# Turning routing scores and the first expert's rows on VectorE instead of TensorE, in a cross-attention and mixture-of-experts kernel

## The chip, the cores and the metric

The kernel runs on one core of a Trainium2 chip. The metric is device time in microseconds (us) of one execution; the time of a kernel is the median of several executions. A profile is one execution taken by the hardware profiler. Its times count from the first instruction, and its span ends with the last one.

The engines are named as the profile names them: PE is TensorE's matmuls and PEld its weight loads, DVE is VectorE, ACT is ScalarE, POOL is GpSimd, and SP is SyncE, which here only issues DMAs. Each engine works through its own instructions in order and waits on semaphores for the others.

## The reference

The kernel computes one transformer block in fp32: `x` is 32 sequences of 100 tokens with 512 features. Cut to what matters:

```python
x = x + xattn(layernorm(x), ctx, ctx)      # 16 heads, causal mask, softmax over the keys, + bias
h = layernorm(x)                           # 3200 tokens x 512
scores = softmax(h @ gate_w.T)             # per token, over 16 experts
topk_w, topk_idx = top_k(scores.T, 12)     # each expert takes its 12 best tokens of each sequence
x_tok = h[topk_idx]
eo = (gelu(x_tok @ Wg.T) * (x_tok @ Wu.T)) @ Wd.T * topk_w     # per expert, hidden size 1024
shared = (gelu(h @ Ws_g.T) * (h @ Ws_u.T)) @ Ws_d.T            # for all tokens
out = x + scatter_add(eo) + shared
```

Because of the causal mask over 100 queries, only the first 100 of 722 context positions matter.

## The kernel before

**Precision.** Every fp32 product of matrices is made of three matmuls. A value is split into a high part (ScalarE copies it to a rounded fp32 type) and a low part (VectorE subtracts the high part from the value), and `mm3` (L49) multiplies high by high, high by low and low by high. So every operand needs one ScalarE and one VectorE instruction before TensorE can use it.

**Attention** runs in 32 units (`u`), four for each of eight blocks of 400 tokens. A unit does, for four heads: the scores of the unit before, the query projection, the turns of the softmax of two units before, a K projection of 384 tokens, in three units out of four also a V projection, and the values of two units before. Units 8, 12 and 16 have no V projection and are shorter on TensorE ("short units"). The softmax passes through VectorE (maxima, L254), GpSimd (subtraction, L263), ScalarE (exponential, L267), VectorE again (sum, L272) and GpSimd (multiplication, L278); ScalarE also copies the turned softmax out (`pt`, L289). The order in each unit is written out by hand in the loop at L543, and each engine keeps it.

Beside that, the four 128-row slices of the output projection's weights are loaded (`load_w`) and split (`fc_split`, L672: L674 on ScalarE, L675 on VectorE), one in each of the units 9 to 12 (`FC_AT`). After them the bias, a table of bases and the router's weights are loaded (`load_consts`, L658, unit 13), and the router's weights are split (`split_consts`, L666, unit 15: L669 and L670).

**Feed-forward** comes next. `job` (L804) runs one expert over up to 384 tokens: eight chunks `f` of the hidden size; in each, `gate_up_mm` (24 matmuls for gate and 24 for up, tile `gu`), then `hidden` (L773 gelu on ScalarE, L774 product on VectorE, L777 and L778 the split of the result), then `down` of the chunk before (tile `dn`). Extra work is hung on a chunk `f`: the list `mid` is issued between gate/up and `down`, the list `post` after `down`. `at(post, 3, ...)` means "after chunk 3's `down`". Within one chunk, calls are issued in the order in which they were added.

First the shared expert runs over eight groups of tokens (`g` from 0 to 7; a ninth group is kept for the end). While a group runs, the next one is prepared (`Prep`): output projection, residual, layer norm, store of the normalized rows to `xn` in DRAM (tensor `xnD`, L1069), turn of the rows so that features lie on partitions (`turn_pe`, L962, four TensorE transposes for 128 rows; or `turn_dve`, L972), and router logits, which end as rows of `LG`, one of 25 tiles of 128 tokens by 16 experts each.

**Routing** (`Route`). In group 6 the softmax over the first 20 tiles is taken after chunk 1. The scores are then turned so that each expert's 3200 scores lie in a row: `turn` (L1191) makes one TensorE transpose for a tile (L1201) and one VectorE copy for up to four of them (L1202), and stores to `sD` in DRAM (L1205). The 20 tiles are spread over chunks 3, 4 and 6 of group 6. The last five tiles get their softmax after chunk 7, and their turn in chunk 0 of group 7. Then `load` (L1213) reads the scores back with 4 rows of 100 for each partition, `top` (L1222 to L1226) finds the 12 best, `exchange` (L1235 to L1242) passes values and indices through DRAM, and `slots` (L1249, L1256) turns them on TensorE into a weight, a row index (`isl`) and a quarter-row index (`iq`) for each slot.

**Experts.** Each of the 16 has 384 slots, in three tiles. `gather` (L934) fetches their rows from `xn`. For the experts after the first this takes four indirect DMAs for each tile, each fetching quarter rows of 128 features (L948), so that the tile arrives as 32-row blocks; `turn_dve` then needs a blockwise 32x32 transpose on VectorE (L979), and the split (L980 on ScalarE, L981 on VectorE). Their three turns are hung on chunks 4, 5 and 6 of the expert before. The first expert's rows come as whole rows (L943, one DMA for each tile) and are turned by TensorE in chunk 7 of group 7 (`turn_pe`, L968, split by L969 and L970). An expert's weights come in eight chunks (`wraw`, L718 on SP), which `chunk_split` splits (L742 on ScalarE, L743 on VectorE) during the expert before. The results are added to the output by indirect DMAs (L991).

Tiles come from pools with a fixed number of buffers: `big` has one, `gx` three. A new tile waits until all uses of the old one are over.

Of the kernel before, what the change touches and what calls it, by code (L numbers as in the profile page):

```python
# [16 lines left out]
T = B * S  # L17
# [8 lines left out]
KSTART = [sum(KVB[:j]) for j in range(len(KVB))]  # L26
KMAX = 384
KS = 1
FC_AT = 9
BUF = dict(cr=4, raw=6, cx=8, x=4, v=2, kk=2, kt=2, vt=2, q=3, p=5, pt=5, y=2, pj=2, sc=1, tr=2)  # L30
GROUPS = [3, 2, 3, 3, 3, 3, 3, 3, 2]
GMAX = 384
# [28 lines left out]
def attention(tc, K, F):  # L61
    nc = tc.nc
    with ExitStack() as ctx, ExitStack() as kvctx:
# [477 lines left out]
        with tc.manual_schedule(engines={mybir.EngineType.Pool}):  # L541
            prologue()
            for u in range(NU - 3):  # L543
                sb, c = divmod(u, NC4)
                a, back = u - 1, u - 2
                a = a if a >= 0 else None
                back = back if back >= 0 else None
                j, ck = divmod(u - KS, NC4)
                j += 2
                kv = j in blocks  # L550
                vv = kv and ck < KVB[j]
                jn, d = divmod(u + NC4 - KS, NC4)
# [12 lines left out]
                if FC_AT <= u < FC_AT + NC4:  # L565
                    fr = load_w(3, u - FC_AT)
                if u == FC_AT + NC4:
                    F.load_consts()
                if u == FC_AT + NC4 + 2:
                    F.split_consts()  # L570
                if a is not None:
                    scores(a)
                if u - 3 >= 0:
                    y_keep(u - 3)
                if a is not None:
                    sm_max(a, 0)
                    sm_sub(a, 0)
                    sm_max(a, 1)
                    sm_sub(a, 1)
                qkeep(u, qproj(u))  # L580
                if a is not None:
                    sm_exp(a, 0)
                if back is not None:
                    p_turn(back, 0)
                    p_turn(back, 1)
                    p_keep(back, 0)
                    p_keep(back, 1)
                if xn:
                    x_stats(*xn)
                if a is not None:  # L590
                    sm_exp(a, 1)
                    sm_sum(a, 0)
                    sm_mul(a, 0)
                pk = kproj(j, ck) if kv else None
                if kv and vv:
                    kkeep(j, ck, pk)
                if c == 1:
                    vload(sb)
                if back is not None:
                    p_turn(back, 2)  # L600
# [12 lines left out]
                if FC_AT <= u < FC_AT + NC4:  # L613
                    F.fc_split(u - FC_AT, fr)
                if u == 0:
                    vkeep(1, 1, vproj(1, 1))
                if vv:
                    vkeep(j, ck, vproj(j, ck))
                if xs:
                    x_turn(sb + 1, c, vv)  # L620
                if back is not None:
                    values(back)
# [8 lines left out]
class FeedForward:  # L631
# [4 lines left out]
    def __init__(self, tc, K, top):  # L636
# [15 lines left out]
        self.sel = self.base[:, 5:5 + NE]  # L652
        self.gr = wfp.tile([128, NC4, 32], F32, name="gr")
        self.gw = wfp.tile([128, NC4, 64], FR, name="gw")
        self.LG = wfp.tile([128, T // 128, NE], F32, name="LG")
        self.stacks = [top.enter_context(ExitStack()) for _ in range(3)]

    def load_consts(self):  # L658
# [3 lines left out]
        nc.gpsimd.memset(gr, 0.0)  # L662
        nc.sync.dma_start(gr[:, :, 0:NE], K.gwT)
        nc.gpsimd.memset(f32(gw), 0.0)

    def split_consts(self):  # L666
        nc, gw, gr = self.nc, self.gw, self.gr
# [150 lines left out]
    def run(self):  # L818
# [10 lines left out]
        for g in range(ng):  # L829
# [58 lines left out]
            if g == ng - 2:  # L888
                n = self.starts[ng - 1]
                at(post, 1, lambda n=n: Route.softmax(self, 0, n))  # L890
                at(post, 3, lambda: r.turn(0, 4), lambda: r.turn(4, 4))
                at(mid, 4, lambda: r.turn(8, 4, True))
                at(mid, 6, lambda: r.turn(12, 4))
                at(post, 6, lambda n=n: r.turn(16, n - 16, True))
                at(post, 7, lambda n=n: Route.softmax(self, n, T // 128))
            if g == ng - 1:
                at(mid, 0, lambda n=n: r.turn(n, T // 128 - n, True))
                at(post, 0, r.load)
                at(post, 1, *[lambda j=j: r.top(j) for j in range(4)], r.exchange)
                at(post, 3, r.slots, lambda: self.gather(0, r))  # L900
                for i in range(NST):
                    at(mid, 7, lambda i=i: self.gturn(0, i))
                for f in range(1, NFC):
                    at(post, f, lambda f=f: self.chunk_split(NFC + f - 1))
            xh, xl, x1s = self.ready.pop(g)
# [28 lines left out]
    def gather(self, e, r):  # L934
# [3 lines left out]
        for j in range(NST):  # L938
            g = self.gxp.tile([128, NC4, 128], F32, name="gx")
            self.gx.append(g)  # L940
            if e == 0:
                nc.gpsimd.indirect_dma_start(
                    out=g.rearrange("p c f -> p (c f)"), out_offset=None, in_=self.K.xn,  # L943
                    in_offset=bass.IndirectOffsetOnAxis(ap=r.isl[:, j:j + 1], axis=0))
                continue
            for k in range(4):
                i = (e * NST + j) * 4 + k
                nc.gpsimd.indirect_dma_start(  # L948
# [4 lines left out]
    def gturn(self, e, j):  # L953
        if j == 0:
            self.xg = self.xt_tiles()
        if e == 0:
            self.turn_pe(self.xg, j, self.gx[j].rearrange("p c f -> p (c f)"),
                         self.ps_m.tile([128, D], F32, name="m").rearrange("p (c t) -> p c t", c=NC4))
        else:
            self.turn_dve(self.xg, j, self.gx[j])  # L960

    def turn_pe(self, x, i, rows, tv):  # L962

# [209 lines left out]
class Route:  # L1173


    def __init__(self, F):
        self.F, self.nc = F, F.nc
        self.so = None

    @staticmethod  # L1180
    def softmax(F, a, b):
# [6 lines left out]
        nc.vector.reciprocal(sm[:, 1], sm[:, 1])  # L1188
        nc.vector.tensor_tensor(LG, LG, sm[:, 1, :, None].to_broadcast([128, NT, NE]), ALU.mult)

    def turn(self, b0, nb, store=False):  # L1191
        F, nc = self.F, self.nc
        if self.so is None:
            self.so = F.bigp.tile([128, NC4, GMAX], F32, name="big").rearrange("p c t -> p (c t)")
            self.at = b0
        for t0 in range(b0, b0 + nb, 4):
            nt = min(4, b0 + nb - t0)
            o = (t0 - self.at) * 128
            tb = F.ps_m.tile([128, D], F32, name="m")
            for i in range(nt):  # L1200
                nc.tensor.transpose(tb[0:NE, i * 128:(i + 1) * 128], F.LG[:, t0 + i, :], F.K.ident)  # L1201
            nc.vector.tensor_copy(self.so[0:NE, o:o + nt * 128], tb[0:NE, 0:nt * 128])  # L1202
        if store:
            n = b0 + nb - self.at
            nc.sync.dma_start(F.K.sD[:, self.at * 128:(self.at + n) * 128],  # L1205
                              self.so[0:NE, 0:n * 128])
            self.so = None

    def load(self):
        F, nc = self.F, self.nc  # L1210
# [122 lines left out]
```

## Time and profile before

| | us |
|---|---|
| median of 3 runs | 1677.03 (1675.21 to 1677.6) |
| the profiled execution | 1675.84 |
| its span | 1674.0 |
| attention, from 62 to 345: PE busy | 279.50 of 283 |
| shared groups, from 345 to 724: PE busy | 376.02 of 379 |
| group 6 from the softmax on, 724 to 776: PE busy | 51.77 of 52 |
| group 7, 776 to 830: PE busy | 52.48 of 54 |
| experts and the late group, 830 to 1674: PE busy | 839.70 of 844 |

The granted TensorE clock is 0.999 over the span. A matmul's duration in the timeline includes the time in which it overlaps with the next one, so the time that a piece of work takes on TensorE is read from the start of the one to the start of the next. In a line of a timeline the columns are start, duration, engine, line, operation, output and inputs, shape, count, and in brackets the idle time of the engine before it and what ended that. In a line of waits the numbers are the total in us, the number of times, and the longest.

### The profile page before, as it was taken

To read this page: it belongs to the slowest core of one execution; us is meant where nothing else is said; L and a number is where in the kernel's file an instruction comes from. 1 tells how busy PE (TensorE), PEld (TensorE's weight loads), DVE (VectorE), ACT (ScalarE), POOL (GpSimd) and SP (SyncE) were. 2 spreads that over 40 slices of the span, in tenths; PEclk is the share of its full clock that TensorE was granted. 3 is DMA by queue.
4 is the path that set the end of the run, shared out by engine and by line. 5 is a ranking of instruction groups with operands and counts; after the bars stand their busy time and mean duration, and the time that the engine had idled before them with its cause. 6 is when DMAs were issued, how large, how long until landed. Compare 5 with 4: busy or idle time off the path is not lost.

```text
span 1674.0 us, 28093 instructions
## 1 busy us (share of the span) xinstructions
PE 1657.8 (99%) x10879; PEld 1523.1 (91%) x10879; DVE 917.9 (55%) x2199; ACT 679.3 (41%) x1088; POOL 625.7 (37%) x542
## 2 busy tenths in 40 slices
PE   9999999999999999999999999999999999999998
PEld 8888899879898999989899999999999999999998
DVE  5778777665433334344555555555555555555542
ACT  4555555553111111122344444444444444444442
POOL 3877777670111011010343344343344343344011
PEclk9999999999999999999999999999999999999999
DMA  7456554555322233211545555455555455555452
GB/s 236 149 166 182 161 164 151 177 181 176 114 70 76 76 101 114 82 45 42 158 163 161 160 157 164 152 152 161 161 155 160 158 150 161 161 155 164 136 160 62
DMA packets 107125, 237.47 MB, mean 142 GB/s; under 512 B 14161, under 2 KB 58418, under 8 KB 106992
## 3 DMA queue, kind: packets, MB, share of 16 engines
q1 hardware_dynamic: 93632, 209.99, 38.4%
q0 software_dynamic: 12944, 25.22, 8.0%
q8 instruction: 85, 1.39, 0.4%
q10 hardware_dynamic: 416, 0.48, 0.1%
q14 instruction: 48, 0.39, 0.1%
HBM read 181.90 MB, written 53.73 MB: 141 GB/s over the span
## 4 chain that ended last, share of the span: by engine, by line
PE 92%; POOL 2%; DVE 2%; ACT 1%; issue 1%; DMA 1%; SPq 0%; POOLq 0%; ACTq 0%; DVEq 0%
PE gu L56 49%; PE dn L56 24%; PE kv L56 10%; PE m L56 3%; PE ms L284 2%; POOL p L263 2%; PE ms L299 2%; PE sc L243 1%; DVE p L254 1%; ACT pt L289 1%; DMA raw<-wA 1%; PE ms L171 0%; DVE y L102 0%; PE m L1112 0%; PE m L968 0%
## 5 line engine op out<-in xcount | busy, mean ns | idle before, releaser
L56 PE MATMUL gu<-xh,whl 128*128 128x384 f32 (+1 forms) x3200 | 642.5, 332 | 0.0
L56 PEld LDWEIGHTS gu<-xh,whl 128*128 128x128 f32 x3200 | 556.6, 188 | 20.0 <-issue 1.9
L56 PE MATMUL dn<-whl,hh 128*128 128x512 f32 x1168 | 366.0, 394 | 0.0
L743 DVE TENSOR_TENSOR whl<-wraw,whl 128x1536 fp32r<-128x1536 f32 x142 | 249.8, 1759 | 203.4 <-ACT whl L742 181.8
L948 POOL DMA_INDIRECT gx<-xnD,iq x180 | 226.9, 1261 | 359.5 <-DVE big L979 299.8
L56 PE MATMUL gu<-xl,whl 128*128 128x384 f32 (+1 forms) x1600 | 336.7, 332 | 0.0
L56 PEld LDWEIGHTS gu<-xl,whl 128*128 128x128 f32 x1600 | 279.9, 188 | 0.0
L777 ACT CAST hh<-g 128x384 fp32r<-128x384 f32 (+1 forms) x200 | 100.9, 505 | 408.6 <-DVE g L774 382.3
L774 DVE TENSOR_TENSOR g<-g,gu 128x384 f32<-128x384 f32 (+1 forms) x200 | 108.3, 542 | 257.5 <-PE gu L56 251.2
L56 PEld LDWEIGHTS dn<-whl,hh 128*128 128x128 f32 x1168 | 215.5, 188 | 36.1 <-ACT hh L777 0.4
L742 ACT CAST whl<-wraw 128x1536 fp32r<-128x1536 f32 x142 | 210.0, 1479 | 61.9 <-PE dn L56 59.0
L56 PE MATMUL dn<-whl,hl 128*128 128x512 f32 x584 | 230.6, 395 | 0.0
L773 ACT ACTIVATE g<-gu 128x384 f32<-128x384 f32 (+1 forms) x200 | 96.3, 481 | 238.0 <-PE gu L56 236.6
L778 DVE TENSOR_TENSOR hl<-g,hh 128x384 fp32r<-128x384 f32 (+1 forms) x200 | 110.7, 554 | 114.2 <-ACT hh L777 113.7
L991 POOL DMA_INDIRECT out_dram<-x,isl x48 | 77.8, 1620 | 171.6 <-ACT x L990 161.9
L56 PEld LDWEIGHTS dn<-whl,hl 128*128 128x128 f32 x584 | 109.7, 188 | 25.3 <-DVE hl L778 0.2
L263 POOL TENSOR_TENSOR p<-p,mx 100x800 f32<-100x800 f32 x64 | 96.7, 1531 | 64.4 <-DVE mx L254 61.3
L278 POOL TENSOR_TENSOR p<-p,sm 100x800 f32<-100x800 f32 x64 | 100.9, 1578 | 6.8 <-DVE sm L273 3.6
L254 DVE CUSTOM_DVE_ANT_0 p<-sc,mask 100x100 f32<-100x100 f32 x512 | 95.4, 256 | 0.0
L1028 POOL TENSOR_TENSOR x<-x,bfc 128x512 f32<-128x512 f32 x23 | 30.9, 1363 | 154.8 <-DMA x<-x 154.6
L980 ACT CAST xh<-big 128x512 fp32r<-128x512 f32 x59 | 36.6, 621 | 101.5 <-DVE big L979 101.5
L272 DVE TENSOR_REDUCE sm<-p 100x8 f32<-100x800 f32 x64 | 63.1, 986 | 25.9 <-ACT p L267 25.9
(161 smaller groups left out, 1636.8 us busy)
## 6 DMA issues: line engine op xcount, KB each, us to landing
wraw<-wE SPq DMA_DIRECT2D x144, 768.0 KB
yD<-y SPq DMA_DIRECT2D x31, 400.0 KB
xt<-x SPq DMA_DIRECT2D x32, 200.0 KB
vD<-vt SPq DMA_DIRECT2D x25, 256.0 KB
kt<-kD SPq DMA_DIRECT2D x32, 200.0 KB
v<-vD SPq DMA_DIRECT2D x8, 800.0 KB
xnD<-xn SPq DMA_DIRECT2D x25, 256.0 KB
out_dram<-x SPq DMA_DIRECT2D x25, 256.0 KB
```

What stands on the lines that cost most here:

```text
L56: r = nc.tensor.matmul(out, t[0][a], t[1][b], start=(first and i == 0), stop=(last and i == n - 1))
L254: nc.vector.tensor_tensor_reduce(out=p[:, bb, h, :], in0=sc[:, h, cs], in1=mask, scale=ISCALE, scalar=NEG, op0=ALU.add, op1=ALU.max, accum ...
L263: nc.gpsimd.tensor_tensor(pv, pv, mx[:, :, None].to_broadcast([S, 8, S]), ALU.subtract)
L278: nc.gpsimd.tensor_tensor(pv, pv, sm[:, :, None].to_broadcast([S, 8, S]), ALU.mult)
L742: nc.scalar.copy(h, r)
L743: nc.vector.tensor_tensor(l, r, f32(h), ALU.subtract)
L773: nc.scalar.activation(g[:, 0:t], pg[:, 0:t], AF.Gelu)
L774: nc.vector.tensor_tensor(g[:, 0:t], g[:, 0:t], pu[:, 0:t], ALU.mult)
L777: nc.scalar.copy(hh[:, 0:t], g[:, 0:t])
L778: nc.vector.tensor_tensor(hl[:, 0:t], g[:, 0:t], f32(hh[:, 0:t]), ALU.subtract)
L948: nc.gpsimd.indirect_dma_start(out=g[:, k, :], out_offset=None, in_=self.K.xn.rearrange("t (a f) -> (t a) f", f=128), in_offset=bass.Indir ...
L991: ins = nc.gpsimd.indirect_dma_start(out=self.K.out, out_offset=bass.IndirectOffsetOnAxis(ap=r.isl[:, i:i + 1], axis=0), in_=o, in_offset= ...
```

## The change

Three things change.

1. **Scores.** `Route.turn` no longer uses TensorE. One VectorE instruction transposes the 32x32 blocks of a stretch of `LG` (two tiles of 16 experts make one block), and eight DMAs, for the four groups of 32 partitions and the two tiles of a block, put the pieces in their places in `sD` in runs of 32 scores. The first 20 tiles are done at once after chunk 3 of group 6, the last five right after their softmax, after chunk 7. `LG` gets a 26th tile, filled with zeros, so that the last block is complete.
2. **First expert.** Its rows are fetched as quarter rows (twelve DMAs in place of three) and turned by `turn_dve` like those of the other experts, one tile after each of chunks 5, 6 and 7 of group 7.
3. **Output weights.** The fourth slice is loaded and split in unit 13 in place of 12; the constants follow in units 14 (was 13) and 17 (was 15).

```diff
-FC_AT = 9
+FC_AT = (9, 10, 11, 13)
...
-                if FC_AT <= u < FC_AT + NC4:
-                    fr = load_w(3, u - FC_AT)
-                if u == FC_AT + NC4:
+                if u in FC_AT:
+                    fr = load_w(3, FC_AT.index(u))
+                if u == FC_AT[-1] + 1:
                     F.load_consts()
-                if u == FC_AT + NC4 + 2:
+                if u == FC_AT[-1] + 4:
                     F.split_consts()
...
-                if FC_AT <= u < FC_AT + NC4:
-                    F.fc_split(u - FC_AT, fr)
+                if u in FC_AT:
+                    F.fc_split(FC_AT.index(u), fr)
...
-        self.LG = wfp.tile([128, T // 128, NE], F32, name="LG")
+        self.LG = wfp.tile([128, T // 128 + 1, NE], F32, name="LG")
...
+        nc.gpsimd.memset(self.LG[:, T // 128], 0.0)
...
-                at(post, 3, lambda: r.turn(0, 4), lambda: r.turn(4, 4))
-                at(mid, 4, lambda: r.turn(8, 4, True))
-                at(mid, 6, lambda: r.turn(12, 4))
-                at(post, 6, lambda n=n: r.turn(16, n - 16, True))
-                at(post, 7, lambda n=n: Route.softmax(self, n, T // 128))
+                at(post, 3, lambda n=n: r.turn(0, n))
+                at(post, 7, lambda n=n: Route.softmax(self, n, T // 128),
+                   lambda n=n: r.turn(n, T // 128))
             if g == ng - 1:
-                at(mid, 0, lambda n=n: r.turn(n, T // 128 - n, True))
                 at(post, 0, r.load)
                 at(post, 1, *[lambda j=j: r.top(j) for j in range(4)], r.exchange)
                 at(post, 3, r.slots, lambda: self.gather(0, r))
                 for i in range(NST):
-                    at(mid, 7, lambda i=i: self.gturn(0, i))
+                    at(post, 5 + i, lambda i=i: self.gturn(0, i))
...
-            if e == 0:
-                nc.gpsimd.indirect_dma_start(
-                    out=g.rearrange("p c f -> p (c f)"), out_offset=None, in_=self.K.xn,
-                    in_offset=bass.IndirectOffsetOnAxis(ap=r.isl[:, j:j + 1], axis=0))
-                continue
             for k in range(4):
...
-        if e == 0:
-            self.turn_pe(self.xg, j, self.gx[j].rearrange("p c f -> p (c f)"),
-                         self.ps_m.tile([128, D], F32, name="m").rearrange("p (c t) -> p c t", c=NC4))
-        else:
-            self.turn_dve(self.xg, j, self.gx[j])
+        self.turn_dve(self.xg, j, self.gx[j])
...
-    def turn(self, b0, nb, store=False):
+    def turn(self, b0, b1):
+
         F, nc = self.F, self.nc
...
+        j0, j1 = b0 // 2, (b1 + 1) // 2
+        so = F.bigp.tile([128, NC4, GMAX], F32, name="big").rearrange("p c t -> p (c t)")
+        nc.vector.transpose(so[:, 0:(j1 - j0) * 32],
+                            F.LG[:, 2 * j0:2 * j1, :].rearrange("p i e -> p (i e)"))
+        sD = F.K.sD.rearrange("e (i a r) -> e i a r", a=4, r=32)
+        for a in range(4):
+            for t in range(2):
+                i = [i for i in range(b0, b1) if i % 2 == t]
+                p, c = 32 * a + NE * t, (i[0] // 2 - j0) * 32
+                nc.sync.dma_start(
+                    sD[:, i[0]:i[-1] + 1:2, a, :],
+                    so[p:p + NE, c:c + len(i) * 32].rearrange("e (j r) -> e j r", r=32))
```

More of the change, by code (lines that the diff above doesn't have):

```diff
@@ L1177, in __init__ @@
         self.F, self.nc = F, F.nc
-        self.so = None
     @staticmethod
@@ L1189, in softmax @@
         nc.vector.tensor_tensor(LG, LG, sm[:, 1, :, None].to_broadcast([128, NT, NE]), ALU.mult)
-    def turn(self, b0, nb, store=False):
+    def turn(self, b0, b1):
         F, nc = self.F, self.nc
[L1193 to L1207, printed above, removed]
+        j0, j1 = b0 // 2, (b1 + 1) // 2
[10 more added lines that the diff above has]
+                    so[p:p + NE, c:c + len(i) * 32].rearrange("e (j r) -> e j r", r=32))
     def load(self):
```

## The prediction

> **What bounds the kernel now.** I read the page's busy row and its chain of waits first, then TensorE's own waits, then the timelines of the three places that the change touches.
>
> ```profile
> span 1674.0 us, 28093 instructions
> PE 1657.8 (99%) x10879; PEld 1523.1 (91%) x10879; DVE 917.9 (55%) x2199; ACT 679.3 (41%) x1088; POOL 625.7 (37%) x542
> ...
> PE 92%; POOL 2%; DVE 2%; ACT 1%; issue 1%; DMA 1%; SPq 0%; POOLq 0%; ACTq 0%; DVEq 0%
> ```
>
> TensorE (PE) is busy 99% of the span, and 92% of the chain is its own work. A microsecond of PE work removed is a microsecond of span, unless a new wait takes its place; work on VectorE (55%) costs nothing until PE waits for it. PE's waits are few, and two of them lie in this change:
>
> ```profile
> PE ms L284 <- ACT pt L289: 2.8, 3, 1.6
> ...
> PE m L968 <- DVE xl L970: 1.5, 1, 1.5
> ```
>
> The longest of the first kind is in attention unit 13, just after the unit (12) in which the last output-weight slice is split. PE's timeline, unit 9 above and unit 13 below (start, duration, and in brackets the idle time):
>
> ```profile
> 120.66 0.86 PE L56 MATMUL kv<-cxh,wl 128*128 128x384 f32 x4
> 121.63 0.94 PE L284 MATMUL ms<-ident,p 100*100 100x100 f32 x8
> ...
> 161.31 0.86 PE L56 MATMUL kv<-cxh,wl 128*128 128x384 f32 x4
> 163.78 0.94 PE L284 MATMUL ms<-ident,p 100*100 100x100 f32 x8 [1.62 <-ACT pt L289]
> ```
>
> Start to start this step takes 0.97 us after a short unit without a slice (0.95 us again in unit 17) and 2.47 us in unit 13. VectorE's timeline has the cause, and the counter-case:
>
> ```profile
> 124.86 1.48 DVE L675 TENSOR_TENSOR wfl<-raw,wfh 128x512 fp32r<-128x512 f32 x1 [0.45 <-ACT wfh L674]
> 126.41 0.57 DVE L102 TENSOR_TENSOR xnl<-ms,xnh 128x400 fp32r<-128x400 f32 x1
> ...
> 156.88 1.48 DVE L675 TENSOR_TENSOR wfl<-raw,wfh 128x512 fp32r<-128x512 f32 x1 [0.45 <-ACT wfh L674]
> ```
>
> Unit 12 has no V projection (about 2.8 us less PE work), so the 1.48 us of L675 delay the next maxima, GpSimd's subtraction and ScalarE's exponentials, and PE arrives first. In unit 9, which has a V projection, the same slice ends just before its successor could start, and PE does not wait.
>
> The other two places are PE's timeline in shared group 6 (score turns) and at the last chunk of group 7 (turns for the first expert):
>
> ```profile
> 744.53 0.39 PE L56 MATMUL dn<-whl,hl 128*128 128x512 f32 x1
> 744.76 0.60 PE L1201 MATMUL m<-ident,LG 128*16 128x128 f32 x4
> 745.59 0.60 PE L1201 MATMUL m<-ident,LG 128*16 128x128 f32 x4 [0.23 <-DVE x L1037]
> 745.95 0.94 PE L56 MATMUL gu<-xh,whl 128*128 128x384 f32 x4
> ...
> 825.28 1.11 PE L968 MATMUL m<-ident,gx 128*128 128x128 f32 x8
> 827.91 0.75 PE L968 MATMUL m<-ident,gx 128*128 128x128 f32 x4 [1.52 <-DVE xl L970]
> 828.42 0.71 PE L56 MATMUL dn<-whl,hh 128*128 128x512 f32 x2
> ```
>
> [...]
>
> **Part 1, score turns: -3.2 us.** All 25 turns leave PE. The first two batches take 745.95 - 744.76 = 1.19 us and slow the gate matmuls after them by 0.09 (0.78 instead of 0.69 us to their next group). A chunk with one row turn and no score turn lasts 6.74 us (753.21 to 759.95); the chunk before it, with one batch, 7.26 less those 0.09, so 0.43; the chunk after it, with two, 7.52, so 0.78, and 0.09 again behind it. In group 7 chunk 0 lasts 6.91 and chunk 1 6.21 us; less 0.11 that the logits' turn leaves there anyway, 0.59. Sum 3.17.
>
> Added on VectorE: blockwise turns of 128x320 and 128x96. The row nearest is L979, 1.095 us for 128x512, so about 0.7 and 0.25 us by size, for seven copies (L1202) of 4.3 us that go. Both fit in VectorE's idle time (1.27 us before the gate product at 750.48, 2.59 us before 780.59), so they cost nothing on the path.
>
> Added on SP: sixteen stores instead of three. An issue of like shape, L1242 (runs of 128 B), takes 0.43 to 0.45 us, so eight take 3.5 us. The first eight (20 tiles) sit at about 749 to 752.5, ahead of two row stores that were issued at 753.79 and that nothing reads before the gathers. The second eight, behind the last softmax at 778.0, are issued by about 782; the three output stores that follow on SP wait for VectorE until about 783. So the load of the scores (L1213, issued at 785.33 behind those stores) is not later. Here a rule speaks against the change: the Trainium skill, "DMA: Bandwidth & Descriptors", Specifications, wants at least 512 B per run, with a read-modify-write below, and its Anatomy section has about 2 us of fixed cost per DMA. Eight in series at 2 us would be 16 us, land at 794.5, and hold the top-8 (789.36) by some 6 us. The row says otherwise: the four L1242 reads are issued from 797.8 to 799.2, and PE uses their data at 802.00, so they overlap. Reads are not writes, so I keep both ends, 0 and +6, and take 0.
>
> **Part 2, first expert's rows: -1.3 us.** Removed: twelve PE turns, 828.42 - 825.28 = 3.14 us with the wait in them, and 0.08 in the next down projection: -3.22. Added: the same VectorE path as the other experts, but a chunk later: they turn tiles in chunks 4, 5, 6, this one in 5, 6, 7. So the third turn stands right before the gate matmuls that read it. One expert's last turn, on VectorE and ScalarE:
>
> ```profile
> 974.94 1.09 DVE L979 STREAM_TRANSPOSE big<-gx 128x512 f32<-128x512 f32 x1
> 976.72 0.69 DVE L981 TENSOR_TENSOR xl<-big,xh 128x512 fp32r<-128x512 f32 x1 [0.69 <-ACT xh L980]
> ```
>
> ```profile
> 976.07 0.62 ACT L980 CAST xh<-big 128x512 fp32r<-128x512 f32 x1 [1.64 <-DVE big L979]
> ```
>
> From turn to end of `xh`: 1.13 + 0.62 = 1.75 us. When does the turn start? Chunk 7's gate matmuls start at 821.08. Two turns earlier, an expert's chunk has its gate product (L774) 4.72 us after that point (968.62 to 973.34; 4.43 without turns), its low half 1.13 later, the turn 0.47 after that: 827.40. `xh` is ready at 829.15. Freed of its turns, PE gets there one chunk after 821.08, at +6.28 (814.80 to 821.08): 827.36. It waits 1.8, with a restart 1.9 us. `xl` is needed four matmuls (0.70) later and is ready then. Net -3.22 + 1.9 = -1.3. Behind the turn on VectorE and ScalarE stands only the split of weight chunk 6, due six chunks later.
>
> The rows must have landed. Twelve gathers of quarter rows replace three of whole rows. An expert's series on GpSimd, first and last:
>
> ```profile
> 863.07 0.94 POOL L948 DMA_INDIRECT gx<-xnD,iq  x1 [19.25 <-DVE big L979]
> ...
> 880.62 1.30 POOL L948 DMA_INDIRECT gx<-xnD,iq  x1 [0.30 <-issue]
> ```
>
> That is 18.85 us (17.6 in the series at 826.19), and the last packets end 3.3 us later in the trace's DMA records. The indices (L1259) are ready at 803.64, so the series runs from 803.9 to 822.8 and lands at 826.0 at worst, before 827.40. By the same records tile 0 lands by 813.7 (turned at 814.6) and tile 1 by 820.1 (turned at 820.9). GpSimd has nothing else; the next expert's gathers queue behind and still start earlier than the 826.19 of before. The bounds of this part are -3.2 (no wait) and about +3 (the last gather 4 us late).
>
> On the wait itself the skill warns: "TensorE: Matmul & The Clock Gate", Part 1, halves the clock after about 3.4 us idle. The trace's 1.62 us gap left the granted clock at 1.00 in the stage. By the rule my 1.9 us is free too, but a wait above 3.4 would add about 2 to 3 us of half-speed matmuls.
>
> **Part 3, slice at unit 13: -1.5 + 0.2 us.** The wait falls to that of other short units: 2.47 - 0.97 = 1.50. Unit 13 has the structure of unit 9, where the slice costs PE nothing (bounds 0 and +0.3). Its load moves on SP with it, behind three other loads and 9 us ahead of use. The constants' loads and two fills on GpSimd (0.21 and 0.31, and a third one of 128x16) go a unit later, before a subtraction that has 2.5 us of idle ahead: 0. But the constants' split goes from unit 15 to the start of 17, behind short unit 16, and there VectorE has no idle time: `xnl` 198.94, `y` 199.43, maxima 199.91. L670 (0.215 us) goes between, so unit 17's wait grows by about 0.2 (bounds 0 and 0.47 with L669).
>
> **Sum.** -3.2 - 1.3 - 1.5 + 0.2 = -5.8. The profiled execution took 1675.84 us (span 1674.0 and 1.84 around it), so 1670.0; it was 1.2 below the median 1677.03, so in the median's terms 1671.2.
>
> **Rivals.**
> A, a smaller gain: the seam waits 1 to 3 us more, because gathers share the DMA with the weight loads from 803 on, or the score chain comes a little late; or unit 13 keeps part of the wait. For: the margins of the gathers are only about 1 us. Against: a late tile 0 or 1 hits a product with 4 us of slack. It gives 1672 to 1675.
>
> B, slower: gathers issued next to the weight splits (L743) get long; the longest is 2.44 us. If all twelve took this with the 0.30 between, the last would end at 836.8 and land at 840.1; PE would wait 12.7 us more and lose some 2 to 3 to the clock. Less the 5.8 this is +9 to +10: 1687. Loss begins where the lateness plus clock exceeds 5.8, so where each issue takes over 1.95 us in place of the 1.57 of the series above. Against: no series in the trace is near that.
>
> C, nothing: VectorE's turns hold PE for as long as its own did, and unit 13 inherits unit 12's wait. That would leave 3.2 - 0.2 = 3.0, within what a measurement of this kernel can tell from no change (0.2%, 3.35 us): 1674.
>
> **Chances.** The sum 75% (1669 to 1673), A 12%, C 5%, B 5%, and 3% for more gain, where the seam hardly waits: 1669 and below. The range 1668.2 to 1674.6 holds the first case, half of A, and C. Faster by over 0.2% means below 1673.7: the sum, the larger gain and most of A, 0.87. Within: 0.08. Slower: 0.05.
>
> **What would show it.** Right: no L1201 row on PE; one PE wait of about 1.9 us for ScalarE's `xh` before the first expert's first gate matmuls; unit 13's step at about 0.97 us, unit 17's at about 1.15. Wrong: a wait of VectorE's third turn for a DMA (B, A), a PE wait at the slot turns (L1249, the stores), or one in unit 14.

## The result, and the profile after

The changed kernel took 1667.27 us (median of five executions, 1666.4 to 1668.93), against 1676.39 us (1675.21 to 1677.6) for the kernel before beside it: a ratio of 0.9947, interval [0.9935, 0.9958], or 9.1 us less. I had forecast 5.8 us less and 1671.2 us, with a range down to 1668.2. The direction was right, the size was not: the median lies 0.9 us below the range. Five more executions later (run e9_again below) had a median of 1668.14, 7.9 us below the kernel before beside them. So the gain to be explained is 8 to 9 us.

The profiled execution of the changed kernel took 1666.98 us. From its page, the span, the busy row and the engines' shares of the chain:

```profile
span 1665.2 us, 28046 instructions
PE 1650.8 (99%) x10842; PEld 1516.6 (91%) x10842; DVE 917.4 (55%) x2197; ACT 678.3 (41%) x1088; POOL 634.9 (38%) x552
...
PE 92%; POOL 2%; DVE 1%; DMA 1%; ACT 1%; issue 1%; SPq 0%; POOLq 0%; ACTq 0%; DVEq 0%
```

PE lost 37 instructions (25 score turns and 12 row turns) and 7.0 us of busy time, the span 8.8 us. PE is the bound as before. Its longest waits (total in us, times, longest):

```profile
PE ms L284 <- ACT pt L289: 2.2, 4, 0.8
PE ms L299 <- ACT pt L289: 2.1, 4, 1.1
PE gu L56 <- ACT xh L969: 1.7, 1, 1.7
```

The wait of 1.6 us in unit 13 has left the first row and the wait for the first expert's turned rows (L968 for `xl`) is gone; the third row is the new wait that I had forecast at 1.8 to 1.9. Now the three places of the change on PE's timeline. Unit 13 and unit 17:

```profile
162.19 0.86 PE L56 MATMUL kv<-cxh,wl 128*128 128x384 f32 x4
163.13 0.94 PE L284 MATMUL ms<-ident,p 100*100 100x100 f32 x8
...
202.76 0.86 PE L56 MATMUL kv<-cxh,wl 128*128 128x384 f32 x4
204.28 0.94 PE L284 MATMUL ms<-ident,p 100*100 100x100 f32 x8 [0.66 <-ACT pt L289]
```

Start to start the step of unit 13 is 0.94 us (2.47 before); that of unit 17 is 1.52 (0.95 before). The score turns and the seam to the first expert:

```profile
744.01 0.86 PE L56 MATMUL gu<-xl,whl 128*128 128x384 f32 x4
744.70 0.86 PE L56 MATMUL gu<-xh,whl 128*128 128x384 f32 x4
745.40 0.63 PE L957 MATMUL m<-ident,xn 128*128 128x128 f32 x4
...
820.58 0.40 PE L56 MATMUL dn<-whl,hl 128*128 128x512 f32 x1
822.67 0.96 PE L56 MATMUL gu<-xh,whl 128*128 128x384 f32 x4 [1.69 <-ACT xh L969]
```

No score turn stands between the gate matmuls and the row turn, and PE waits once at the seam, for ScalarE's high half. The scores' stores on SP (start, duration of the eight issues together):

```profile
744.94 3.66 SPq L1191 DMA_DIRECT2D sD<-big  x8
...
772.39 3.59 SPq L1191 DMA_DIRECT2D sD<-big  x8
```

They take 3.6 us for eight, as costed (3.5), and nothing waits for them.

**Where the 8.8 us between the two spans lie.** I took the starts of ScalarE's exponentials (attention) and gelus (feed-forward) in both traces as landmarks, and read how the distance between them changed. The last column is the profile of e9_again, the same kernel profiled a second time.

| stretch | forecast | profile after | second profile |
|---|---|---|---|
| start of the kernel to unit 1 | 0 | +1.02 | -1.28 |
| step of unit 13 | -1.50 | -1.53 | -1.52 |
| step of unit 17 | +0.2 | +0.57 | +0.57 |
| the other units | 0 | -0.01 | +0.46 |
| handover from attention to feed-forward (325 to 358) | 0 | -2.76 | -0.08 |
| shared groups, to 711 | 0 | -0.69 | -0.69 |
| score turns (groups 6 and 7) | -3.17 | -3.22 | -3.22 |
| seam to the first expert | -1.3 | -1.17 | -1.20 |
| experts, 833 to the end | 0 | -1.01 | -1.04 |
| sum | -5.8 | -8.80 | -8.00 |

The edited places do what the working said. Four stretches that nobody edited do not stay at zero. Two of them differ between two profiles of one kernel (the start and the handover). The other two rows, shared groups and experts, are the same to 0.03 us in both, and together they are worth 1.7. Of the experts' row, 0.37 lies behind the last group's last gelu: VectorE's last product (L774; L775 after) sits idle 3.23 us before it starts in the kernel before and 2.91 in the changed one. The value is 2.88 to 2.91 in all seven profiles of kernels with part 2, and 3.23 to 3.26 in the six without; why part 2 does this isn't shown.

### The profile page after: what moved, and what is told of

It reads as the page before. It is cut to its first block, busy times and chain, and to the rows that moved or that the text cites. A ratio compares the mean times of both kernels' runs of the same rounds, so it can differ in the third digit from the quotient of the medians.

```text
span 1665.2 us, 28046 instructions
## 1 busy us (share of the span) xinstructions
PE 1650.8 (99%) x10842; PEld 1516.6 (91%) x10842; DVE 917.4 (55%) x2197; ACT 678.3 (41%) x1088; POOL 634.9 (38%) x552
## 4 chain that ended last, share of the span: by engine, by line
PE 92%; POOL 2%; DVE 1%; DMA 1%; ACT 1%; issue 1%; SPq 0%; POOLq 0%; ACTq 0%; DVEq 0%
PE gu L56 49%; PE dn L56 24%; PE kv L56 10%; PE m L56 3%; PE ms L284 2%; PE ms L299 2%; POOL p L263 1%; PE sc L243 1%; DMA raw<-wA 1%; DVE p L254 0%; ACT pt L289 0%; PE ms L171 0%; POOL p L278 0%; PE m L1101 0%; DMA xt<-x 0%
## 5 line engine op out<-in xcount | busy, mean ns | idle before, releaser
L941 POOL DMA_INDIRECT gx<-xnD,iq x192 | 241.3, 1257 | 401.5 <-DVE big L968 303.6
L775 DVE TENSOR_TENSOR g<-g,gu 128x384 f32<-128x384 f32 (+1 forms) x200 | 108.3, 542 | 255.3 <-PE gu L56 249.0
L774 ACT ACTIVATE g<-gu 128x384 f32<-128x384 f32 (+1 forms) x200 | 96.2, 481 | 233.1 <-PE gu L56 232.4
L278 POOL TENSOR_TENSOR p<-p,sm 100x800 f32<-100x800 f32 x64 | 101.0, 1580 | 5.4 <-DVE sm L273 3.6
```

What stands on the lines that cost most here:

```text
L278: nc.gpsimd.tensor_tensor(pv, pv, sm[:, :, None].to_broadcast([S, 8, S]), ALU.mult)
L774: nc.scalar.activation(g[:, 0:t], pg[:, 0:t], AF.Gelu)
L775: nc.vector.tensor_tensor(g[:, 0:t], g[:, 0:t], pu[:, 0:t], ALU.mult)
L941: nc.gpsimd.indirect_dma_start(out=g[:, k, :], out_offset=None, in_=self.K.xn.rearrange("t (a f) -> (t a) f", f=128), in_offset=bass.Indir ...
```

## The experiments

### Which part brings what: e1_slice, e2_scores, e3_rows, e4_noslice

The first three put one part alone on the kernel before. The fourth takes part 3 out of the changed kernel:

```diff
-FC_AT = (9, 10, 11, 13)
+FC_AT = 9
...
-                if u == FC_AT[-1] + 4:
+                if u == FC_AT + NC4 + 2:
                     F.split_consts()
```

> The kernel before with part 3 alone: the fourth weight slice in unit 13, constants in units 14 and 17. All theories: the step of unit 13 falls from 2.47 to about 0.95 us, that of unit 17 rises from 0.95 to about 1.5, together -0.9 us. Theory 1 (the slice's move shifts the later units against their loads and fills, and so the meeting of VectorE's norm and GpSimd's multiplications at the handover to the feed-forward): norm L1058 at 337 takes about 1.8 us in place of 3.21, no PE wait above 2 us at about 348, the granted clock 1.00 throughout, and about 3.6 us less than the kernel before, near 1672.5. Theory 2 (the handover goes one way or the other by chance, whatever was changed): the wait and the half clock may be there or not; the time is 0.5 to 1.5 below the kernel before if its median has the same share of both. Theory 3 (the score turns or the first expert's rows gain more than their places show): about 0.9 less, near 1675.3, with the long norm and the half clock as before.

> The kernel before with part 1 alone: the scores turned by VectorE, eight stores a time, LG's 26th tile filled. Attention is unchanged but for one fill of 128x16 on GpSimd. All theories: -3.2 us at the turns. Theory 1 (slice moves the handover): the long norm (about 3.2 us) and a half clock stay; time 3.2 below the kernel before, near 1673.2. Theory 2 (chance): 3.2 below, or up to 2.7 more where a profile has the short norm. Theory 3: 5 or more below, with no change in attention.

> The kernel before with part 2 alone: the first expert's rows as quarter rows, turned by VectorE in chunks 5 to 7. All theories: -1.3 us at the seam, a PE wait of 1.7 us for ScalarE's high half. Theory 1: the handover as before (norm about 3.2 us, half clock for some 3.4 us), time 1.3 below the kernel before, near 1675. Theory 2: 1.3 below, up to 2.7 more by chance. Theory 3: 3 or more below.

> The changed kernel with part 3 undone: the fourth slice back in unit 12, the constants in 13 and 15; scores and rows as changed. Theory 1 (the slice's move brought the gain at the handover): it loses 0.9 at units 13 and 17 and 2.7 at the handover, so 3.6 above the changed kernel, near 1671, with the norm at about 3.2 us and a half clock after it. Theory 2 (chance): 0.9 above, near 1668.2, the handover one way or the other. Theory 3: 0.9 above, near 1668.2, with the handover slow as in the kernel before.

Measured, with the kernel before at 1676.09 us beside them:

| kernel | median | ratio to before, interval |
|---|---|---|
| e1_slice | 1675.01 | 0.999 [0.9983, 0.9997] |
| e2_scores | 1670.01 | 0.9964 [0.9952, 0.9976] |
| e3_rows | 1675.17 | 0.9988 [0.9981, 0.9995] |
| e4_noslice | 1669.16 | 0.9957 [0.9943, 0.997] |

Part 3 alone gives 1.1 us and part 2 alone 0.9, about what their places show (0.95, and 1.2 without the 0.37 at the end). So theory 1 falls: the slice's move does not bring the rest. e4_noslice lies 1.5 above the changed kernel's ten executions (1667.7), where part 3's places are 0.95. Part 1 alone gives 6.1, where its place shows 3.2. That is theory 3's direction for the scores. And the landmarks say where: in the profiles of e2_scores and e4_noslice two successive experts take 100.25 us, in those of e1_slice and e3_rows 100.36, as in the kernel before. (The expectations of e5, e6 and e11 below call this length "an expert". It is two: eight chunks of about 6.27 us make one expert of about 50.2, and a chunk has 24 gate and up matmuls, 12 for each.) So the slow drift over the feed-forward comes with part 1, though part 1 edits nothing there.

At the handover, the profiles fit theory 2: the changed kernel alone shows both outcomes. There VectorE's norm of a row tile (L1058; L1047 after) starts just as GpSimd begins two multiplications (L278). VectorE's timeline, kernel before and after:

```profile
337.19 3.21 DVE L1058 TENSOR_SCALAR xn<-x,mv,rs 128x512 f32<-128x512 f32 x1
```

```profile
337.38 1.82 DVE L1047 TENSOR_SCALAR xn<-x,mv,rs 128x512 f32<-128x512 f32 x1
```

GpSimd's two, in the kernel before and after:

```profile
337.11 3.01 POOL L278 TENSOR_TENSOR p<-p,sm 100x800 f32<-100x800 f32 x2
```

```profile
337.31 3.27 POOL L278 TENSOR_TENSOR p<-p,sm 100x800 f32<-100x800 f32 x2
```

The same norm takes 0.55 us in the groups. Here it ends 0.28 us after GpSimd's second multiplication, or 0.37 after the first, and then GpSimd's two take 0.26 us longer. The Trainium skill, "SBUF — State Buffer", "Who interferes with whom", says why that can be: a `tensor_scalar` can need a pair of ports that a GpSimd instruction needs too, whoever issues first gets the pair for the whole instruction, and the other blocks. The trace agrees with the blocking; it does not show the ports. Which of the two ends the norm gets differs from profile to profile: 1.82 in the changed kernel and in e2_scores, 3.2 in the kernel before, e1, e3 and e4, and 3.20 in the second profile of the changed kernel. In the ten profiles with this norm on VectorE the two short ones started 0.077 us after GpSimd's first multiplication, the eight long ones 0.081 to 0.090 us after it. Some nanoseconds may decide, then; ten profiles don't show it.

### The tile that nobody counted: e5_pad, e6_nopad, e11_pad2

Part 1 has an edit that I priced as one fill on GpSimd: a 26th tile in `LG`. It adds 16 fp32 values, 64 B, to each partition of the weights' pool, so pools opened after it on the same side (those of `open_first`) should lie elsewhere; the traces hold no addresses. e5_pad has that and nothing else; e11_pad2 adds 128 B (`+ 2` in place of `+ 1`):

```diff
-        self.LG = wfp.tile([128, T // 128, NE], F32, name="LG")
+        self.LG = wfp.tile([128, T // 128 + 1, NE], F32, name="LG")
...
+        nc.gpsimd.memset(self.LG[:, T // 128], 0.0)
```

e6_nopad is the changed kernel without it. The second score turn starts a tile earlier, so that its blocks are complete:

```diff
-        j0, j1 = b0 // 2, (b1 + 1) // 2
+        s0 = b0 - b1 % 2
+        nb = (b1 - s0) // 2
...
-                            F.LG[:, 2 * j0:2 * j1, :].rearrange("p i e -> p (i e)"))
+                            F.LG[:, s0:b1, :].rearrange("p i e -> p (i e)"))
...
```

> The kernel before with only the 26th tile of LG and its fill: 64 B more in the weights' pool, so every pool opened later lies 64 B elsewhere, and one fill of 128x16 more on GpSimd; nothing is turned otherwise. Theory A (the place of the tiles in SBUF makes matmuls of the feed-forward a little faster): an expert takes 100.26 in place of 100.36 us, the shared groups 360 to 710 lose about 0.7, together 1.5 to 1.6 us below the kernel before, near 1674.5. Theory B (the score turns themselves, or the order of work behind them, speed the experts up): 100.36 us for each expert and no difference, near 1676. Theory C (the place also decides the wait and the half clock at the handover to the feed-forward): 3 to 4 us below, near 1672.5, with a granted clock of 1.00 at 350.

> The changed kernel without the 26th tile: the second turn takes tiles 19 to 24, so its blocks are complete, and every pool lies where it lay in the kernel before. Theory A (place): an expert takes 100.36 us again; 1.5 above the changed kernel, near 1668.8. Theory B: 100.26 us, near 1667.3. Theory C (place decides the handover too): the half clock at 350 comes back in most runs; 3 to 4 above, near 1671.

> The kernel before with two more tiles in LG, 128 B, in place of one (64 B). If any shift of the tiles makes the feed-forward's matmuls faster, an expert takes 100.26 us as in e5_pad, 1.6 below the kernel before. If it is the place within 128 B that counts, an expert takes 100.36 us as in the kernel before, and there is no difference.

Measured: e5_pad 1674.32 us, ratio 0.9989 [0.9981, 0.9997] (kernel before 1676.14, so -1.8); e6_nopad 1670.91, ratio 0.9964 [0.9949, 0.9979]; e11_pad2 1678.2, ratio 1.0012 [1.0004, 1.0019] (kernel before 1675.99, so +2.2). The gelu of the first chunk of three successive experts, on ScalarE's timelines. Kernel before:

```profile
1184.27 0.49 ACT L773 ACTIVATE g<-gu 128x384 f32<-128x384 f32 x1 [0.66 <-PE gu L56]
...
1234.40 0.49 ACT L773 ACTIVATE g<-gu 128x384 f32<-128x384 f32 x1 [0.69 <-PE gu L56]
...
1284.63 0.49 ACT L773 ACTIVATE g<-gu 128x384 f32<-128x384 f32 x1 [0.66 <-PE gu L56]
```

e5_pad, the tile alone:

```profile
1183.44 0.49 ACT L774 ACTIVATE g<-gu 128x384 f32<-128x384 f32 x1 [0.70 <-PE gu L56]
...
1233.62 0.49 ACT L774 ACTIVATE g<-gu 128x384 f32<-128x384 f32 x1 [0.67 <-PE gu L56]
...
1283.69 0.49 ACT L774 ACTIVATE g<-gu 128x384 f32<-128x384 f32 x1 [0.70 <-PE gu L56]
```

e6_nopad, the changed kernel without it:

```profile
1180.92 0.49 ACT L773 ACTIVATE g<-gu 128x384 f32<-128x384 f32 x1 [0.66 <-PE gu L56]
...
1231.05 0.49 ACT L773 ACTIVATE g<-gu 128x384 f32<-128x384 f32 x1 [0.69 <-PE gu L56]
...
1281.28 0.49 ACT L773 ACTIVATE g<-gu 128x384 f32<-128x384 f32 x1 [0.66 <-PE gu L56]
```

e11_pad2, two tiles:

```profile
1186.83 0.49 ACT L774 ACTIVATE g<-gu 128x384 f32<-128x384 f32 x1 [0.70 <-PE gu L56]
...
1237.18 0.49 ACT L774 ACTIVATE g<-gu 128x384 f32<-128x384 f32 x1 [0.67 <-PE gu L56]
...
1287.43 0.49 ACT L774 ACTIVATE g<-gu 128x384 f32<-128x384 f32 x1 [0.70 <-PE gu L56]
```

Two experts take 100.36 us in the kernel before, 100.25 with 64 B more, 100.36 again when the changed kernel lies where the old one lay, and 100.60 with 128 B more. In e5_pad's profile this makes 0.8 over the sixteen experts, of which the late group gives 0.2 back; with 0.7 over the shared groups and 0.1 around the score turns it is 1.4 in all. 128 B cost 0.24 for two experts. Theory A holds as far as the padding goes, theory B (the turns themselves speed the experts up) falls, and for e11_pad2 both of my expectations fall: the next step of the same kind turns the gain into a loss.

The single experts take turns: 50.13 and 50.23 us in the kernel before, 50.19 and 50.07 with 64 B more, 50.35 and 50.25 with 128 B more, and every profile with the same padding repeats its pair to 0.01 us. So 64 B make one expert slower and the next one faster, and the 0.11 is what is left. The program also uses two buffers for an expert's rows in turn (`xt_tiles`), one opened in `open_first` and one in `open_rest`; no run tests whether that is the link.

Theory C falls in its strict form: e5_pad has the tile, the long norm (3.20 us) and a half clock at 350. A weaker form, that the tile makes full-clock executions more frequent, is not excluded. Counted afterwards, the mean granted clock is 1.000 in 19 of 35 executions of the kernels with 64 B more and the norm on VectorE (changed kernel, e2, e4, e5), and in 40 of 139 of those without (kernel before, e1, e3, e6). e6_nopad came 1.4 us above what theory A alone gives (the changed kernel at 1667.7 over all ten executions, and 1.8), near the 1671 of theory C. Its two executions at 1.000 took 1667.17 and 1668.24; the other five, at lower clocks, 1670.15 to 1673.1.

What in the place counts isn't shown. The lost time lies in the matmuls themselves: over two experts' 384 gate and up matmuls PE's busy time goes the same way (windows of 100 us from 1183, the tile `gu` alone; kernel before, e5_pad, e11_pad2):

```profile
1183.00:1283.00 100.00, 69.23 (x384) 67.06 (x383) 8.83 (x16) 7.83 (x16) 1.00 0.54 157
```

```profile
1183.00:1283.00 100.00, 69.17 (x384) 67.00 (x384) 8.83 (x16) 7.82 (x16) 1.00 0.55 158
```

```profile
1183.00:1283.00 100.00, 69.55 (x384) 67.49 (x384) 8.82 (x16) 7.81 (x16) 1.00 0.53 158
```

The first number after the length is PE's busy time, the second that of the weight loads. VectorE and ScalarE (third and fourth) spend the same time on that tile, and the granted clock is 1.00 in all three.

### The handover by itself: e7_norm, e8_both, e9_again

e7_norm moves that one norm to ScalarE in the kernel before, with a 128x1 instruction on GpSimd for its bias:

```diff
+    def shift(self, i):
+        mv, rs = self.mv[i]
+        self.F.nc.gpsimd.tensor_scalar(mv[:, 0:1], mv[:, 0:1], rs, -1.0, ALU.mult, ALU.mult)
+    def norm_act(self, i):
+        mv, rs = self.mv[i]
+        xn = self.F.xnp.tile([128, D], F32, name="xn")
+        self.F.nc.scalar.activation(xn, self.xb[i], AF.Identity, bias=mv[:, 0:1], scale=rs)
+        self.xn[i] = xn
...
             pr.rsqrt(0)
+            pr.shift(0)
...
-            pr.norm(0)
+            pr.norm_act(0)
```

e8_both does this to the changed kernel, and moves `split_consts` from unit 17 to 18 (`FC_AT[-1] + 5`). e9_again is the changed kernel, as it is.

> The kernel before with the norm of the first row tile in the handover (L1058 at 337) on ScalarE in place of VectorE, and one more 128x1 instruction on GpSimd for its bias; nothing else. If the norm on VectorE waits there for GpSimd's two multiplications, and TensorE's wait of 2.3 us and the half clock at 350 follow from that: VectorE is free 1.4 to 3.2 us earlier, TensorE waits about 0.9 us at 348, the clock stays 1.00 there, and the profile shows the handover (exponentials 58 to 62) in about 21.2 us in place of 24.24; the median falls by 2 to 3, to 1673 to 1674, with less spread. If the half clock there has another cause, it stays, and the median falls by 1.4 at most.

> The changed kernel with that norm on ScalarE, and the constants' split in unit 18 in place of 17. Split: the step of unit 17 falls from 1.52 back to about 0.95 us, -0.5. Norm: about -0.3 against the changed kernel's profiled run (its norm took 1.82 us), and up to -3 in executions where it took 3.2 us. So 1665.5 to 1666.7. If the changed kernel's gain at the handover came from the change and not by chance, only the -0.5 to -0.8 is there; if by chance, the spread is smaller than 1666.4 to 1668.9.

> The changed kernel itself once more. The parts by their places in the trace (slice and unit 17 -0.9, score turns -3.2, seam -1.3) and the place of the tiles (-1.65) make 7.05; the kernel before is at 1676.1 by now, which leaves 1669.0. If the rest of its gain (9.1 in five executions) was a lucky draw at the handover to the feed-forward, the new executions have a median of 1668.5 to 1669.5 and some of them lie above 1669, and the profile may show the long norm and a half clock at 350. If the rest belongs to the change, the median is 1667.3 again.

Measured: e7_norm 1674.82 us, ratio 0.9991 [0.9983, 0.9999], 1.3 less; e8_both 1666.29, ratio 0.9939 [0.9924, 0.9953]; e9_again 1668.14 (1667.44 to 1668.77), ratio 0.9953 [0.994, 0.9967]. PE at the handover in the kernel before, in the changed kernel, in its second profile, and in e7_norm:

```profile
348.39 0.89 PE L299 MATMUL ms<-pt,v 100*32 100x100 f32 x32 [2.30 <-ACT pt L289]
...
351.29 2.08 PE L56 MATMUL kv<-wfh,yh 128*128 128x512 f32 x4
```

```profile
347.19 0.89 PE L299 MATMUL ms<-pt,v 100*32 100x100 f32 x32 [1.09 <-ACT pt L289]
...
349.59 1.20 PE L56 MATMUL kv<-wfh,yh 128*128 128x512 f32 x4
```

```profile
346.53 0.89 PE L299 MATMUL ms<-pt,v 100*32 100x100 f32 x32 [2.31 <-ACT pt L289]
...
349.27 2.08 PE L56 MATMUL kv<-wfh,yh 128*128 128x512 f32 x4
```

```profile
347.82 0.89 PE L299 MATMUL ms<-pt,v 100*32 100x100 f32 x32 [1.14 <-ACT pt L289]
```

A long norm delays the maxima, GpSimd's subtraction, the exponentials and `pt` by 1.2 us, and PE waits 2.3 us in place of 1.1. After a 2.3 us wait the same four matmuls (`wfh,yh`) take 2.08 in place of 1.20, because the granted clock falls to half. Windows of four us, the clock in the third column from the end, kernel before and after:

```profile
350.00:354.00 4.00, 4.00 (x39) 3.30 (x40) 3.89 (x22) 1.50 (x3) 2.59 (x4) 0.57 0.33 117
```

```profile
350.00:354.00 4.00, 3.61 (x23) 2.89 (x22) 3.97 (x33) 1.19 (x3) 2.90 (x4) 1.00 0.48 177
```

So the long norm costs 1.2 us of wait and, mostly, some 1.5 of half-speed matmuls. (In e3, e6 and e11 the half clock lasted twice as long, 6.8 us.) That is the -2.76 of the first profile, and e9_again shows it at -0.08 in the same kernel: the changed kernel doesn't always have this gain, and whether it has it more often is left open above. With the norm on ScalarE the profile of e7_norm has the short wait, the clock at 1.00, and the handover 2.7 us shorter than in the kernel before. Its median falls by only 1.3, below the 2 to 3 that I expected: not every execution of the kernel before pays the whole price, and other draws remain (its executions still spread from 1672.73 to 1676.53). In e8_both the split takes 0.217 us in unit 18 in place of 0.651, unit 17's step is back to the kernel before's (its change from there is +0.01 us in place of +0.57), and the median is 1.0 below the changed kernel's first five executions; its six executions, 1665.03 to 1668.37, spread no less than the changed kernel's, against that expectation.

### A better version: e10_seam

e10_seam is e8_both with the first expert's third turn one step earlier:

```diff
-                for i in range(NST):
+                for i in range(NST - 1):
                     at(post, 5 + i, lambda i=i: self.gturn(0, i))
                 for f in range(1, NFC):
                     at(post, f, lambda f=f: self.chunk_split(NFC + f - 1))
+                at(post, 6, lambda: self.gturn(0, NST - 1))
```

> As e8_both (norm of the first row tile in the handover on ScalarE, constants' split in unit 18), and the first expert's third turn one step earlier: after chunk 6's weight split in place of after chunk 7's down projection, so before chunk 7's product on VectorE. If TensorE's wait at the seam (1.69 us) is only for this turn and its high half, and the rows have landed by 820.8, the wait goes: 1.7 below e8_both, near 1664.6. If the rows are later, VectorE waits for a DMA there and holds chunk 7's product, which TensorE needs only 6 us later: still about -1.7. If the turn's place moves the wait to the next product or split, the gain is below 1.

Measured: 1663.28 us (1662.85 to 1665.54), ratio 0.9927 [0.9913, 0.994]. That is 12.7 us below the kernel before and, in other runs, 4.4 below the median of the changed kernel's ten executions (1667.7). Below e8_both it is 3.0, more than the 1.7 expected; the places in the two profiles give 1.6, and the rest is not placed. VectorE's timeline shows the turn before the product of chunk 7 (L776), and PE's the seam without a wait:

```profile
818.27 1.08 DVE L970 STREAM_TRANSPOSE big<-gx 128x512 f32<-128x512 f32 x1
820.04 0.69 DVE L972 TENSOR_TENSOR xl<-big,xh 128x512 fp32r<-128x512 f32 x1 [0.69 <-ACT xh L971]
820.65 0.55 DVE L776 TENSOR_TENSOR g<-g,gu 128x384 f32<-128x384 f32 x1
```

```profile
819.57 0.40 PE L56 MATMUL dn<-whl,hl 128*128 128x512 f32 x1
820.06 0.96 PE L56 MATMUL gu<-xh,whl 128*128 128x384 f32 x4
```

The rows had landed (VectorE shows no wait for a DMA), and chunk 7's product has the slack: the first expert now starts 0.49 us after the last down matmul's start in place of 2.09. The wait that I accepted as the price of part 2 was a matter of order.

## Why the prediction was right and where it was wrong

**Part 1, the turns: right.** Forecast -3.17, found -3.22 in both profiles (0.1 of it is the tile's place: e5_pad, without the new turns, has -0.10 in this stretch). VectorE's two turns took 0.51 and 0.28 us (estimates 0.7 and 0.25), inside its idle time. The cost that spoke against the eight stores, about 2 us fixed for each, did not add up in series: eight issues took 3.66 us, the load of the scores was issued at 778.57, and no engine waited for it. The value taken, 0, was right.

**Part 2, the first expert: right.** Forecast -1.3, found -1.17 and -1.20; the new wait is 1.69 us where I had 1.8 to 1.9. The gathers' series was issued from 797.03 to 815.35, 18.3 us (I took 18.85), and none of the turns waited for its rows. The 0.37 us at the last product, which comes with this part, was not foreseen. Rivals A, B and C did not come. (B's 836.8 counts twelve gaps between twelve issues; with eleven it is 836.5.)

**Part 3: right at unit 13, mis-sized at unit 17.** Unit 13: -1.53 for -1.50. Unit 17: +0.57 for +0.2. The term was the split of the router's weights at its duration in unit 15, 0.215 us. In unit 17 it runs beside GpSimd's work and took three times as long:

```profile
L671 DVE TENSOR_TENSOR gw<-gr,gw x1: 651/651/651, 198.7 to 198.7; 128x64 fp32r<-128x64 f32 x1
```

My upper bound, 0.47, was too low too, because it was made of durations from another neighbourhood.

**The step that failed is in part 1: what `LG`'s 26th tile adds.** I counted its fill (0) and never its place. The tile alone is worth 1.8 us by the medians (1.2 among executions with a clock of 1.000, 1674.82 against 1673.63) and 1.4 by the places in its profile; with the tile out of the changed kernel, the drift over the shared groups and experts is gone. The sum is then -5.8 + 0.4 (unit 17) - 1.4 (tile) - 0.4 (last product) = -7.2, against -7.05 for the rows of the table without the start, the other units and the handover. The tile by itself would have moved the forecast to between 1669.4 and 1669.8, still inside my range. That the first five executions lie below the range has a second cause, in the next two paragraphs.

**The rest is not settled to the last microsecond.** Ten executions of the changed kernel have a median of 1667.7, 8.4 below the 90 of the kernel before (about 1676.1). So some 1.3 us are open, with an uncertainty of several tenths. Half-clock stretches are a candidate: 26 of 90 executions of the kernel before have a mean granted clock of 1.000, and 5 of 10 of the changed kernel (4 of the first five, 1 of the second). Among these alone the medians are 1674.82 and 1667.27, 7.6 apart, which is near the places' 7.1; so most of the open part goes with the clock. So few executions do not show whether the change has fewer half clocks (theory C's weaker form) or had fewer by luck. The first five executions' 9.1 had the more full-clock executions, the second five's 7.9 the fewer.

**The sum's footing was also at fault.** I took one profiled execution and assumed that every place outside the edits would repeat, and started from 1677.03, the median of three executions, where 90 have 1676.1. That profile's mean clock of 0.999 was a sign: it is one half-clock stretch of 3.4 us behind a 2.30 us wait, which I had overlooked when I wrote that a wait is free below 3.4 us. The rival for more gain got 3%, with a cause (the seam hardly waits) that was not the one that came.

## What to carry to other kernels

Count the memory that a change adds, not only its instructions: where TensorE is busy 99% of the time, 64 B more in an early pool made the later experts 0.1% faster in the mean and 128 B made them 0.24% slower, so build a control with the padding alone before giving the difference to an idea. A VectorE instruction can take its duration from its neighbours: beside GpSimd's work the two instructions here took three to six times their quiet time, so price a moved instruction at the place where it will run. Where a turn or split is the last thing before its reader, look for its input's arrival and move it ahead of work with slack, as e10_seam did for 1.6 us.

## What the hardware showed that I had not expected

- TensorE's time for the same matmuls changed with padding in an earlier pool: 100.36, 100.25 and 100.60 us for two experts with 0, 64 and 128 B more, the clock at 1.00 in the stretches shown. "SBUF — State Buffer", "Who interferes with whom", in the Trainium skill says that TensorE never waits on anyone there. These runs show the time and not what it is spent on, so whether they contradict that is open.
- A wait well below 3.4 us can be followed by a half clock. In eight profiles PE waited 2.14 to 2.31 us at the handover, and a half clock followed in all but e4_noslice (2.17 us, clock 1.00). The waits of 0.68 to 1.25 us there, of 1.6 us in unit 13 and of 1.7 us at the seam were never followed by one; one of 1.65 us at 7.8 us in e3_rows was. By the traces' clock records the half clock lasts 3.41 us, or 6.83 in e3, e6 and e11, and every stretch between two changes of the clock is a whole number of 3.41 us. These windows cut e4's wait into 1.16 and 1.00 us; ahead of the seven half clocks at the handover, PE was idle for 1.45 to 2.31 us of a window. As other windows with 1.5 to 1.7 us of idle passed without one, no threshold comes out. "TensorE: Matmul & The Clock Gate", Part 1, describes a window of about 3.4 us that runs freely; the lengths fit, the idle time needed was shorter than a window here.
- Which of GpSimd's two multiplications the norm waits for is not fixed by the kernel: 1.82 us in one profile of the changed kernel and 3.20 in the other, for the same instruction.
